# Order of the inner products, place of layer 2's constants, and an earlier branch flag in a four-layer fp32 kernel

## The chip, the cores and the metric

The kernel runs on one core of one Trainium2 chip. The metric is the time of one execution on the device in microseconds (us). A core has several engines, each with a queue that it works through in order: TensorE (PE in the profile) multiplies matrices, with its weight loads listed apart (PEld); VectorE (DVE), ScalarE (ACT) and GpSimd (POOL) work elementwise; SyncE (SP) here starts transfers. SBUF is the memory on the core that all of them read and write; PSUM holds what TensorE produces, in eight banks of 128 partitions x 512 fp32 words.

## What is computed

The input is a batch of 8 images with 512 channels of 32 x 32 positions, in fp32. Four layers follow each other:

```python
# layer 0: group norm, 8-head attention, three steps of an inner loop, projection
h = group_norm(x); q, k, v = split(qkv_w @ h + qkv_b)
hf = softmax(q.T k * 64 ** -0.5) @ v                  # per head, 64 channels
for _ in range(3):
    hf = hf + 0.1 * tanh(hf @ inl_w.T + inl_b)
x = x + proj_w @ hf + proj_b
# layer 1: one head, 64-wide q and k, 512-wide v
x = x + v1 @ softmax(q1.T k1).T
# layer 2: add bias, filter up by 2 (12 taps), leaky relu, filter down by 2 (12 taps)
x = down(leaky_relu(up(x + bias)) * sqrt(2))
# layer 3: 8 experts mixed per image, 1x1, 3x3 and 1x1 convolution with norms, relu, residual
x = relu(bn(conv1(relu(bn(conv3(relu(bn(conv1(x)))))))) + x)
```

## The kernel before

**Stages.** One program does everything. Layers 0 to 2 run image by image, with the result of layer 2 put aside in device memory; then layer 3 runs for all eight images. The Python code emits instructions in program order, and a scheduler then fixes the order in each engine's queue from that order of emission and from costs of its own. The kernel before and the changed one therefore differ in the queues by more than the lines edited. Whatever lies behind a waiting instruction in the queue of its engine waits with it.

**Products.** Each multiplication of a 512 x 512 weight with a 512 x 1024 activation (q, k, v, three inner steps `inl_0` to `inl_2`, proj in layer 0; v1 in layer 1: eight an image) is done in `product` (L382) in Strassen and Winograd's form: seven products of half the size, called P1, C11, U2, U3, C22, C21 and C12, instead of eight. The sums of activation quarters that it needs (tiles `T_...`) come from DVE in `quarter_sums` (L363), the sums of weight quarters from GpSimd in `weight_sums` for image 0, which also stores them for later images. Each of the seven is made in two halves, u = 0 and 1, of one PSUM bank each. P1 and C11 go into the pair of banks A (two tiles of one bank), the others into X (U2, U3, C21) and Y (C22, C12), each of which is one tile of two banks with the tag "scores". TensorE's matmuls for all of this are at L414. After both halves, `made` is called for each; it emits what takes the result out of PSUM:

- `channels` for q and k (ACT and DVE), `positions` for v and v1 (L478 to L495, with the adds of U2 and U3 to P1 at L488),
- `inner_step` for the inner loop: P1 is copied by ACT (L514), U2 and U3 are added to P1 by DVE (L519), C22, C21 and C12 are added to these (L523), ACT takes tanh (L508), and DVE adds a tenth of it to `hf` (L505),
- `residual` for proj, which adds into `x`.

`product` is a generator that yields after each of the seven; a caller can put other work between them.

**Attention in layer 0.** For each group of two heads and half of the positions, TensorE makes scores (L264: two matmuls of 64 rows each, r = 0 and 1, on the two halves of the array's rows), ACT the exponentials `e` (L613), DVE their running sum `acc` (L619), TensorE the weighted sum `av` (L628) and the column totals `total` (L638); DVE takes the reciprocal (L642) and multiplies it into `hf` (L643). GpSimd adds `acc` and `inv` into a tile `seen` (L645). The last of eight groups ends just before the first inner product, which needs its `hf`.

**Layer 1.** The first two parts of v1's product go out first, then the score matmuls (L264) two tiles at a time, with one more part of v1 after each:

```python
for steps in ((0,), (1, 2), (3, 4), (5, 6), (7,)):
    for t in steps:
        scores(t)
    next(values)
```

The exponentials are at L717; the weighted sum is a product of the same kind (L853, evacuated at L827), whose code the change does not touch.

**Layer 2's constants.** The filters are matmuls (L919 up, L940 down) with constant operators `up_op`, `up_left_op`, `dn_op`, `up63_op` and `dn63_op`. `layer2_constants()` (L132) makes them on the core out of the 12 taps, in some 370 small DVE instructions on tiles of 1 to 128 columns (L154 to L190), all in one scratch tile `setup`. It is called once, in layer 1 of image 0.

**The pools.** PSUM's eight banks are three pools: `ps_sc` (two tiles of two banks, the tag "scores"), `ps_tp` and `ps_mm` (two banks each). In SBUF the tag "tmp" has four buffers that the raw weight blocks of `weight` (`raw_kv`, `raw_inl`, `raw_proj`, ...), the exponentials and the tiles that hold P1, U2 and U3 share.

**The flag.** The softmax is computed without subtracting a maximum. At the end of the program `seen` is compared with a bound (L1167 to L1175), the count of values within it gives the flag `redo`, and the engines load it and branch: if it is set, the whole sequence runs again with shifts. In these runs it is not set.

Of the kernel before, what the change touches and what calls it, by code (L numbers as in the profile page):

```python
# [9 lines left out]
F32 = mybir.dt.float32  # L10
# [43 lines left out]
def tile_sequence(ctx: ExitStack, tc: tile.TileContext, a: dict, out: bass.AP, shifted: bool):  # L54
# [77 lines left out]
    def layer2_constants():  # L132

        setup = big_tile("setup", [P, CC * S])
        used = [0]

        def scratch(name, n):
            used[0] += n
            return setup[:, used[0] - n : used[0]]

        def iota(name, pattern, base, per_partition=0):
            t = scratch(name, pattern[0][1])
            nc.gpsimd.iota(
                t, pattern, base=base, channel_multiplier=per_partition,
                allow_small_or_imprecise_dtypes=True,
            )
            return t

        def placed(name, idx, taps):
            n = idx.shape[1]  # L150
            t, one = scratch(f"placed_{name}", n), scratch(f"one_{name}", n)
            for k in range(NTAP):
                dst = t if k == 0 else one
                nc.vector.tensor_scalar(  # L154
                    dst, idx, float(k), taps[:, k : k + 1], ALU.is_equal, ALU.mult
                )
                if k:
                    nc.vector.tensor_add(t, t, one)
            return t

        taps_up = scratch("taps_up", NTAP)
        nc.gpsimd.dma_start(taps_up, a["up_filter"].partition_broadcast(P))
        nc.vector.tensor_scalar_mul(taps_up, taps_up, 2.0)
        taps_dn = scratch("taps_dn", NTAP)
        nc.gpsimd.dma_start(taps_dn, a["down_filter"].partition_broadcast(P))

        part = iota("part", [[1, 1]], 0, 1)

        def rows_of(name, width):

            row, step = scratch(f"row_{name}", 1), scratch(f"step_{name}", 1)
            nc.vector.memset(row, 0.0)
            for k in range(width, P, width):
                nc.vector.tensor_scalar(step, part, float(k), None, ALU.is_ge)
                nc.vector.tensor_add(row, row, step)
            col = scratch(f"col_{name}", 1)
            nc.vector.scalar_tensor_tensor(col, row, float(-width), part, ALU.mult, ALU.add)
            return row, col

        def tap_index(name, n, step, base, mul, by):  # L180

            t = iota(f"ix_{name}", [[step, n]], base)
            add = scratch(f"add_{name}", 1)
            nc.vector.tensor_scalar_mul(add, by, float(mul))
            nc.vector.tensor_scalar_add(t, t, add)
            return t

        def outer(op, rows, cols):
            nr, ncol = rows.shape[1], cols.shape[1]
            nc.vector.tensor_tensor(  # L190
                op.rearrange("p (r c) -> p r c", c=ncol),
                rows.unsqueeze(2).to_broadcast([P, nr, ncol]),
                cols.unsqueeze(1).to_broadcast([P, nr, ncol]),
                ALU.mult,
            )

        in_c, in_r = rows_of("in", IR)
        ur = placed("ur", tap_index("ur", UR, -1, 17, -2, in_r), taps_up)
        outer(up_op, ur, placed("uc", tap_index("uc", UC, 1, 11, -2, in_c), taps_up))
        outer(
            up_left_op, ur, placed("ucl", tap_index("ucl", UC, 1, 11 - 2 * EDGE, -2, in_c), taps_up)
        )
        up_rr, up_cc = rows_of("up", UC)  # L210
        outer(
            dn_op,
            placed("dr", tap_index("dr", OR, 2, -6, 1, up_rr), taps_dn),
            placed("dc", tap_index("dc", OC, 2, 0, -1, up_cc), taps_dn),
        )
        in_c, in_r = rows_of("in63", 3)
        outer(
            up63_op,
            placed("ur63", tap_index("ur63", 1, 0, 10, -2, in_r), taps_up),
            placed("uc63", tap_index("uc63", 2 * W, 1, 5, -2, in_c), taps_up),  # L220
        )
        outer(
            dn63_op,
            placed("dr63", iota("dr63", [[2, 3]], 1), taps_dn),
            placed("dc63", tap_index("dc63", W, 2, 6, -1, part), taps_dn),
        )

        rim0 = tmp("rim0")
        nc.vector.memset(rim0, 0.0)
        for t in ypad:  # L230
            nc.gpsimd.dma_start(t[0 : 3 * W], rim0[0 : 3 * W])
            nc.gpsimd.dma_start(t[(H + 3) * W :], rim0[0 : 2 * W])
# [146 lines left out]
            nc.vector.tensor_sub(t[3][cc], t[1][cc], b21)  # L379
        return t  # L380

    def product(name, wt, src, sums_of, made, rows=False):  # L382

        banks = {
            "A": [bank(name=f"{name}_A{u}") for u in range(2)],
        }
        for key in "XY":
            two = ps_sc.tile([P, S], F32, tag="scores", name=f"{name}_{key}")  # L390
            banks[key] = [two[:, ts(u, HALF)] for u in range(2)]
# [6 lines left out]
        for what, key, part, data in order:  # L398
            part = wt[:, PARTS.index(part)]
            if isinstance(data, int):  # L400
                data = sums_of[data]
            else:
                data = [data[:, cc] for cc in range(2)]
            opens = what in ("P1", "U2", "C22")
            for u in range(2):
                ps = banks[key][u]
                for s in range(2 if rows else 1):
                    for cc in range(2):
                        if rows:
                            at = (2 * u + s) * P  # L410
                            dst, lhs, rhs = ps[:, ts(s, QR)], data[cc][:, at : at + P], part[:, cc]
                        else:
                            dst, lhs, rhs = ps, part[:, cc, ts(u, P)], data[cc]
                        nc.tensor.matmul(  # L414
                            dst, lhs, rhs, start=(opens and s == 0 and cc == 0),
                            stop=(cc == 1 and s == rows), skip_group_check=True,
                        )
            for u in range(2):
                made(what, u, banks[key][u])
            yield  # L420

    def all_of(gen):
        for _ in gen:
            pass
# [141 lines left out]
    def layer0(b, x, norm, w):  # L566
        h = group_norm(b, x, *norm)
        t = quarter_sums(f"h_{b}", h)
        if b == 0:
            for key in "kv":  # L570
                w[key] = weight_sums(key, *held[key], t[3][1][:, 0:1])
        q = big_tile(f"q_{b}", [P, CC, S])
        k = big_tile(f"k_{b}", [P, CC, S])
        v = big_tile(f"v_{b}", [P, SC, C])
# [73 lines left out]
        for t in range(0, n + 4, 2):  # L648
            for u in (t, t + 1):
                if u < n:  # L650
                    scores(u)
            for u in (t - 2, t - 1):
                if 0 <= u < n:
                    weighted(u)
            if t >= SC + 2 and (t - 2) % SC == 0:
                normalised((t - 2) // SC - 1)

        for it in range(3):
            t = quarter_sums(f"hf_{b}_{it}", hf, None if it else v)
            name = f"inl_{b}_{it}"  # L660
            all_of(product(name, w["inl"], hf, t, inner_step(name, hf)))
        if b + 1 < B:
            w["q"] = weight("q", b + 1)
        t = quarter_sums(f"hf_{b}_3", hf)
# [4 lines left out]
    def layer1(b, x, w, midway):  # L669
# [29 lines left out]
            )  # L699
        v = big_tile(f"v1_{b}", [P, SC, C])  # L700
        eT = [big_tile(f"eT_{b}_{sh}", [P, SC, HALF]) for sh in range(2)]
        if b == 0:
            layer2_constants()
        inv = small.tile([P, SC], F32, tag="inv1", bufs=2, name=f"inv1_{b}")
        accs = {}

# [31 lines left out]
            nc.gpsimd.tensor_add(seen[:, 0:4], seen[:, 0:4], inv[:, at])  # L738

        values = product(f"v1_{b}", w["v1"], x, t_x, positions(f"v1_{b}", v), rows=True)  # L740
        for _ in range(2):
            next(values)
        for steps in ((0,), (1, 2), (3, 4), (5, 6), (7,)):
            for t in steps:
                scores(t)
            next(values)
            if 4 in steps:
                totals(0)
        all_of(values)
# [336 lines left out]
    def mixed(b):  # L1086
# [10 lines left out]
                )  # L1097
        return wt

    z3 = {}  # L1100

    def freed(t):
# [8 lines left out]

    z_last = layer2(B - 1, halo, freed)
    z_next = z3[0]
    wt_next = mixed(0)
    route(B - 1, B)
    for b in range(B):
# [28 lines left out]
        for oc in range(CC):  # L1145
# [8 lines left out]
            for part in range(S // n):  # L1154
# [2 lines left out]
                    dst, ps[:, ts(part, n)], bn[2][0][:, oc : oc + 1], dst, ALU.mult, ALU.add  # L1157
                )
                nc.scalar.activation(dst, dst, AF.Relu, bias=bn[2][1][:, oc : oc + 1])
            nc.sync.dma_start(out[b, ts(oc, P), :], z[:, oc, :])  # L1160

    if shifted:
        return None

    within = tmp("within")  # L1167
    nc.vector.tensor_scalar(within, seen, BOUND, None, ALU.is_le)
    count = small.tile([P, 1], F32, tag="count", name="count")
    nc.vector.tensor_reduce(count, within, AX.X, ALU.add)  # L1170
    ps = bank(name="within")
    nc.tensor.matmul(ps[0:1, 0:1], count, ones[:, 0:1], start=True, stop=True)
    redo = small.tile([P, 1], mybir.dt.int32, tag="redo", name="redo")
    nc.vector.tensor_scalar(redo[0:1, :], ps[0:1, 0:1], P * HALF - 0.5, None, ALU.is_lt)
    return nc.values_load(redo[0:1, 0:1], min_val=0, max_val=1)  # L1175


def _layout(inp):
# [64 lines left out]
```

## Time and profile before

| what | value |
|---|---|
| time, median of 3 runs | 3966.25 us (3964.2 to 3972.21) |
| span of the profiled run | 3956.6 us |
| TensorE busy | 3873.8 us, 98% |
| VectorE busy | 2592.0 us, 66% |
| ScalarE busy | 1104.7 us, 28% |
| GpSimd busy | 437.9 us, 11% |
| DVE on `setup` (L154, L158, L174, L175), first and last start | 330.8 to 397.2 us |
| GpSimd's weight sums for proj, first and last start | 67.57 to 72.74 us |
| k of image 0, image 1, image 2 begins at | 43.45, 522.30, 978.89 us |

A line of the list of waits reads: engine, operation and line that waited, what it waited for, then the total in us, how many times, and the longest. A line of the timeline reads: start in us, length in us, engine, line, operation, output and inputs, shape, number of instructions drawn together, and in brackets the idle time of the engine before it and what ended it. An fp32 matmul of the program appears as two records. A line of the view of one tile reads: count, then the shortest, median and longest duration in ns, then the first and the last start.

### The profile page before, as it was taken

To read this page: it belongs to the slowest core of one execution; us is meant where nothing else is said; L and a number is where in the kernel's file an instruction comes from. 1 tells how busy PE (TensorE), PEld (TensorE's weight loads), DVE (VectorE), ACT (ScalarE), POOL (GpSimd) and SP (SyncE) were. 2 spreads that over 40 slices of the span, in tenths; PEclk is the share of its full clock that TensorE was granted. 3 is DMA by queue.
4 is the path that set the end of the run, shared out by engine and by line. 5 is a ranking of instruction groups with operands and counts; after the bars stand their busy time and mean duration, and the time that the engine had idled before them with its cause. 6 is when DMAs were issued, how large, how long until landed. Compare 5 with 4: busy or idle time off the path is not lost.

```text
span 3956.6 us, 37918 instructions
## 1 busy us (share of the span) xinstructions
PE 3873.8 (98%) x14630; PEld 2036.0 (51%) x14630; DVE 2592.0 (66%) x3690; ACT 1104.7 (28%) x1507; POOL 437.9 (11%) x310
## 2 busy tenths in 40 slices
PE   8998999999999999999999999999999999999998
PEld 4335753476435763367434764357534764346543
DVE  4779548764676647765486646765477655766885
ACT  1421214212332114212241223322142123321332
POOL 5310003000120003100030002200030001201000
PEclk9999999999999999999999999999999999999999
DMA  5002310113101310023101220013200131003432
GB/s 189 19 7 78 105 71 1 40 62 114 38 1 59 117 59 19 0 83 114 56 1 58 75 85 36 0 69 107 78 1 24 61 115 54 1 0 115 159 140 95
DMA packets 85214, 247.85 MB, mean 63 GB/s; under 512 B 10416, under 2 KB 32960, under 8 KB 78240
## 3 DMA queue, kind: packets, MB, share of 16 engines
q1 hardware_dynamic: 69136, 220.23, 15.6%
q10 hardware_dynamic: 13824, 12.59, 0.9%
q0 software_dynamic: 2064, 12.51, 0.8%
q8 instruction: 117, 1.92, 0.2%
q14 instruction: 73, 0.60, 0.0%
HBM read 185.40 MB, written 59.90 MB: 62 GB/s over the span
## 4 chain that ended last, share of the span: by engine, by line
PE 91%; DVE 6%; ACT 1%; DMA 1%; issue 1%; POOL 0%; ACTq 0%; SPq 0%; DVEq 0%; POOLq 0%
PE scores L264 13%; PE av L628 11%; PE inl_X L414 6%; PE dn L940 6%; PE up L919 5%; PE v_X L414 4%; PE inl_Y L414 4%; PE av_X L853 4%; PE inl_A L414 3%; PE c L1135 3%; PE v_Y L414 3%; PE av_Y L853 3%; PE av_A L853 2%; PE proj_X L414 2%; PE q_X L414 2%; PE k_X L414 2%
## 5 line engine op out<-in xcount | busy, mean ns | idle before, releaser
L613 ACT ACTIVATE e<-scores 128x1024 f32<-128x1024 f32 x512 | 497.4, 1022 | 583.0 <-PE scores L264 580.3
L619 DVE TENSOR_TENSOR acc<-acc,e 128x1024 f32<-128x1024 f32 x384 | 494.0, 1287 | 123.5 <-ACT e L613 103.4
L264 PE MATMUL scores<-q,k 64*128 64x512 f32 x2048 | 511.1, 616 | 6.0 <-DVE v L495 3.3
L628 PE MATMUL av<-e,v 128*64 128x512 f32 x2048 | 494.2, 605 | 0.0
L645 POOL TENSOR_TENSOR seen<-seen,acc 128x512 f32<-128x512 f32 x128 | 213.6, 1669 | 1565.0 <-DVE acc L619 1560.0
L264 PEld LDWEIGHTS scores<-q,k 64*128 64x128 f32 x2048 | 176.0, 186 | 333.1 <-ACT e L613 162.1
L628 PEld LDWEIGHTS av<-e,v 128*64 128x64 f32 x2048 | 124.9, 136 | 338.7 <-issue 336.4
L903 DVE SCALAR_TENSOR_TENSOR up<-up,leak 128x512 f32<-128x512 f32 (+1 forms) x264 | 174.5, 686 | 141.8 <-ACT leak L902 136.5
L940 PEld LDWEIGHTS dn<-dn_op,up 128*128 128x128 f32 (+1 forms) x2048 | 240.2, 192 | 44.0 <-issue 24.2
L940 PE MATMUL dn<-dn_op,up 128*128 128x126 f32 (+5 forms) x2048 | 244.7, 275 | 7.6 <-DVE up L903 6.8
L642 DVE RECIPROCAL inv<-total 128x512 f32<-128x512 f32 x64 | 214.7, 3355 | 0.0
L902 ACT ACTIVATE leak<-up 128x512 f32<-128x512 f32 (+1 forms) x264 | 150.1, 595 | 208.2 <-DVE up L903 131.0
L414 PE MATMUL inl_A<-hf,w_inl 128*128 128x512 f32 x384 | 178.0, 599 | 10.7 <-DVE hf L643 10.7
L919 PE MATMUL up<-halo,up_op 126*128 126x512 f32 (+1 forms) x384 | 182.6, 604 | 0.9 <-DVE up L903 0.8
L414 PE MATMUL inl_X<-T_hf,w_inl 128*128 128x512 f32 x384 | 175.2, 592 | 0.0
L645 POOL TENSOR_TENSOR seen<-seen,inv 128x512 f32<-128x512 f32 x64 | 125.2, 1956 | 416.9 <-DVE inv L642 416.9
L617 DVE TENSOR_TENSOR acc<-e,e 128x1024 f32<-128x1024 f32 x64 | 83.0, 1297 | 102.5 <-ACT e L613 102.5
L508 ACT ACTIVATE inl_U<-inl_U,inl_b 128x512 f32<-128x512 f32 x96 | 66.7, 718 | 287.4 <-DVE inl_U L523 287.4
L519 DVE TENSOR_TENSOR inl_U<-inl_X,inl_P 128x512 f32<-128x512 f32 x96 | 61.8, 685 | 111.4 <-PE inl_X L414 111.4
L737 POOL TENSOR_TENSOR seen<-seen,acc 128x512 f32<-128x512 f32 x16 | 23.4, 1461 | 987.7 <-DVE acc L729 921.5
L414 PEld LDWEIGHTS inl_A<-hf,w_inl 128*128 128x128 f32 x384 | 70.4, 190 | 110.2 <-issue 95.3
L1135 PE MATMUL c<-rim,mixed 128*128 128x512 f32 x288 | 124.9, 592 | 0.0
(302 smaller groups left out, 5779.0 us busy)
## 6 DMA issues: line engine op xcount, KB each, us to landing
halo<-ypad_u SPq DMA_DIRECT2D x128, 252.0 KB
halo<-ypad_u SPq DMA_DIRECT2D x128, 198.0 KB
w_v<-stored_u_v SPq DMA_DIRECT2D x14, 1792.0 KB
x<-in_x_dram SPq DMA_DIRECT2D x32, 512.0 KB
out_dram<-z SPq DMA_DIRECT2D x32, 512.0 KB
spill_u<-z SPq DMA_DIRECT2D x28, 512.0 KB
z<-spill_u SPq DMA_DIRECT2D x28, 512.0 KB
w_q<-stored_u_q SPq DMA_DIRECT2D x7, 1792.0 KB
```

The costliest lines, as they stand in the source:

```text
L264: nc.tensor.matmul(ps[r], k[r], q[r], start=True, stop=(shift is None))
L414: nc.tensor.matmul(dst, lhs, rhs, start=(opens and s == 0 and cc == 0), stop=(cc == 1 and s == rows), skip_group_check=True,)
L613: nc.scalar.activation(e, ps, AF.Exp, scale=HD ** -0.5)
L619: nc.vector.tensor_add(accs[g], accs[g], e)
L628: nc.tensor.matmul(avs[g][rows[r]], v[:, jc, ts(2 * oc + r, HD)], e[:, ts(r, HALF)], start=(jc == 0), stop=(jc == SC - 1),)
L642: nc.vector.reciprocal(inv, ps)
L645: nc.gpsimd.tensor_add(seen, seen, part)
L853: nc.tensor.matmul(ps[:, ts(s, QR)], left[:, j, at : at + P], right[:, j, :], start=(what in ("P1", "U2", "W") and s == 0 and j == 0), sto ...
L903: nc.vector.scalar_tensor_tensor(dst, ps, SQRT2, t, ALU.mult, ALU.max)
L919: nc.tensor.matmul(ps[i], op[0 : IR * n, :], halo.tile(t)[0 : IR * n, c + i, :], start=True, stop=True,)
L940: nc.tensor.matmul(rows[:, r0 - first : r1 + 1 - first, c0 : c1 + 1], up[t][0:k, c, ts(cc, P)], op[:, r0 - 4 * t + 3 : r1 + 4 - 4 * t, c0 ...
L1135: nc.tensor.matmul(banks[g].rearrange("p (h w) -> p h w", w=W), wt[:, at : at + P], h1[:, ky + 16 * g : ky + 16 * g + 16, kx : kx + W], st ...
```

## The change

There are four parts.

1. The first inner product of an image gets its pair of banks A from `ps_mm` and `ps_tp`, and its first half is emitted ahead of the totals of the last attention group (`normalised`), so that TensorE has work while the last sum and reciprocal are made.
2. In `product`, `made` is called after each half, and the generator yields after each half; only C12 still takes both of its halves at its end. Layer 1's loop takes twice as many steps of the generator, so that as many parts lie between its scores as before.
3. `layer2_constants()` works on GpSimd instead of DVE and is called in layer 0 of image 0, right after the sums of the weights of k and v, so that DVE is free in layer 1.
4. The flag `redo` is computed and loaded before layer 3 instead of after it; the stores of the output go out for each part as it is ready (halves for the last image, whole rows of 1024 for the others, as before).

```diff
@@ layer2_constants: all of its small operations @@
-                nc.vector.tensor_scalar(
+                nc.gpsimd.tensor_scalar(
                     dst, idx, float(k), taps[:, k : k + 1], ALU.is_equal, ALU.mult
                 )
                 if k:
-                    nc.vector.tensor_add(t, t, one)
+                    nc.gpsimd.tensor_add(t, t, one)
...
             for k in range(width, P, width):
-                nc.vector.tensor_scalar(step, part, float(k), None, ALU.is_ge)
-                nc.vector.tensor_add(row, row, step)
+                nc.gpsimd.tensor_scalar(step, part, float(k), None, ALU.is_ge)
+                nc.gpsimd.tensor_add(row, row, step)
...
-            nc.vector.scalar_tensor_tensor(col, row, float(-width), part, ALU.mult, ALU.add)
+            nc.gpsimd.tensor_scalar_mul(col, row, float(-width))
+            nc.gpsimd.tensor_add(col, col, part)
...
@@ product @@
-        banks = {
-            "A": [bank(name=f"{name}_A{u}") for u in range(2)],
-        }
+        banks = {"A": first_banks or [bank(name=f"{name}_A{u}") for u in range(2)]}
...
-            for u in range(2):
-                made(what, u, banks[key][u])
-            yield
+
+                for v in {"C12": ((), (0, 1))[u]}.get(what, (u,)):
+                    made(what, v, banks[key][v])
+                yield
@@ layer0 @@
                 w[key] = weight_sums(key, *held[key], t[3][1][:, 0:1])
+            layer2_constants()
...
-            if t >= SC + 2 and (t - 2) % SC == 0:
+            if t >= SC + 2 and (t - 2) % SC == 0 and t < n + 2:
                 normalised((t - 2) // SC - 1)
...
-            t = quarter_sums(f"hf_{b}_{it}", hf, None if it else v)
-            name = f"inl_{b}_{it}"
-            all_of(product(name, w["inl"], hf, t, inner_step(name, hf)))
+            name, t = f"inl_{b}_{it}", []
+            banks = None if it else [bank(p, f"{name}_A{u}") for u, p in enumerate((ps_mm, ps_tp))]
+            step = product(name, w["inl"], hf, t, inner_step(name, hf), first_banks=banks)
+            if it == 0:
+                next(step)
+                normalised(len(groups) - 1)
+            t += quarter_sums(f"hf_{b}_{it}", hf, None if it else v)
+            all_of(step)
@@ layer1 @@
-        if b == 0:
-            layer2_constants()
...
-        for _ in range(2):
+        for _ in range(4):
             next(values)
...
-            next(values)
+            for _ in range(2):
+                next(values)
@@ layer 3 @@
     z_next = z3[0]
+    redo = None if shifted else out_of_bounds()
...
-            nc.sync.dma_start(out[b, ts(oc, P), :], z[:, oc, :])
+                nc.sync.dma_start(out[b, ts(oc, P), ts(part, n)], dst)
```

`out_of_bounds` holds the comparison, the count and the load of the flag that stood at the end; its matmul writes to a bank of `ps_tp`.

More of the change, by code (lines that the diff above doesn't have):

```diff
@@ L162, in layer2_constants @@
         nc.gpsimd.dma_start(taps_up, a["up_filter"].partition_broadcast(P))
-        nc.vector.tensor_scalar_mul(taps_up, taps_up, 2.0)
+        nc.gpsimd.tensor_scalar_mul(taps_up, taps_up, 2.0)
         taps_dn = scratch("taps_dn", NTAP)
@@ L171, in rows_of @@
             row, step = scratch(f"row_{name}", 1), scratch(f"step_{name}", 1)
-            nc.vector.memset(row, 0.0)
+            nc.gpsimd.memset(row, 0.0)
             for k in range(width, P, width):
-                nc.vector.tensor_scalar(step, part, float(k), None, ALU.is_ge)
-                nc.vector.tensor_add(row, row, step)
+                nc.gpsimd.tensor_scalar(step, part, float(k), None, ALU.is_ge)
+                nc.gpsimd.tensor_add(row, row, step)
             col = scratch(f"col_{name}", 1)
-            nc.vector.scalar_tensor_tensor(col, row, float(-width), part, ALU.mult, ALU.add)
+            nc.gpsimd.tensor_scalar_mul(col, row, float(-width))
+            nc.gpsimd.tensor_add(col, col, part)
             return row, col
@@ L183, in tap_index @@
             add = scratch(f"add_{name}", 1)
-            nc.vector.tensor_scalar_mul(add, by, float(mul))
-            nc.vector.tensor_scalar_add(t, t, add)
+            nc.gpsimd.tensor_scalar_mul(add, by, float(mul))
+            nc.gpsimd.tensor_scalar_add(t, t, add)
             return t
@@ L189, in outer @@
             nr, ncol = rows.shape[1], cols.shape[1]
-            nc.vector.tensor_tensor(
+            nc.gpsimd.tensor_tensor(
                 op.rearrange("p (r c) -> p r c", c=ncol),
@@ L228, in layer2_constants @@
         rim0 = tmp("rim0")
-        nc.vector.memset(rim0, 0.0)
+        nc.gpsimd.memset(rim0, 0.0)
         for t in ypad:
@@ L380, in quarter_sums, with product @@
         return t
-    def product(name, wt, src, sums_of, made, rows=False):
-        banks = {
-            "A": [bank(name=f"{name}_A{u}") for u in range(2)],
-        }
+    def product(name, wt, src, sums_of, made, rows=False, first_banks=None):
+        banks = {"A": first_banks or [bank(name=f"{name}_A{u}") for u in range(2)]}
         for key in "XY":
@@ L1098, in mixed, with out_of_bounds @@
         return wt
+    def out_of_bounds():
+        within = tmp("within")
+        nc.vector.tensor_scalar(within, seen, BOUND, None, ALU.is_le)
+        count = small.tile([P, 1], F32, tag="count", name="count")
+        nc.vector.tensor_reduce(count, within, AX.X, ALU.add)
+        ps = bank(ps_tp, "within")
+        nc.tensor.matmul(ps[0:1, 0:1], count, ones[:, 0:1], start=True, stop=True)
+        redo = small.tile([P, 1], mybir.dt.int32, tag="redo", name="redo")
+        nc.vector.tensor_scalar(redo[0:1, :], ps[0:1, 0:1], P * HALF - 0.5, None, ALU.is_lt)
+        return nc.values_load(redo[0:1, 0:1], min_val=0, max_val=1)
     z3 = {}
@@ L1159, in tile_sequence @@
                 nc.scalar.activation(dst, dst, AF.Relu, bias=bn[2][1][:, oc : oc + 1])
-            nc.sync.dma_start(out[b, ts(oc, P), :], z[:, oc, :])
[L1162 to L1175, printed above, removed]
+                nc.sync.dma_start(out[b, ts(oc, P), ts(part, n)], dst)
+    return redo
 def _layout(inp):
```

## The prediction

> **What bounds the kernel now.** I read the busy shares first, then the chain that ended last, then the waits of TensorE, and last the timeline around each place that the change touches.
>
> ```profile
> PE 3873.8 (98%) x14630; PEld 2036.0 (51%) x14630; DVE 2592.0 (66%) x3690; ACT 1104.7 (28%) x1507; POOL 437.9 (11%) x310
> PE 91%; DVE 6%; ACT 1%; DMA 1%; issue 1%; POOL 0%; ACTq 0%; SPq 0%; DVEq 0%; POOLq 0%
> PE gn_mean L286 <- DVE mv L280: 10.9, 1, 10.9
> PE inl_A L414 <- DVE hf L643: 10.7, 7, 1.5
> PE v_X L414 <- DVE setup L174: 9.0, 1, 9.0
> PE total L638 <- DVE acc L619: 8.6, 8, 1.1
> ```
>
> TensorE is busy for 98% of the span: 3956.6 - 3873.8 = 82.8 us idle in all. Every other engine has room; GpSimd is idle for 89%. So a change gains only what it takes out of those 82.8 us, or out of matmul time, and loses whatever new gap it opens on TensorE. The three waits that the change aims at (10.7, 8.6, 9.0, each line: total, times, longest) can be seen in the list.
>
> How tight matmuls follow is needed below. These lines give start, length, engine, line and operation, and in brackets the idle time before:
>
> ```profile
> 727.50 6.17 PE L414 MATMUL inl_A<-hf,w_inl 128*128 128x512 f32 x14
> 727.70 1.29 DVE L523 TENSOR_TENSOR inl_U<-inl_Y,inl_U 128x512 f32<-128x512 f32 x2
> 732.09 0.68 DVE L377 TENSOR_TENSOR T_hf<-hf,T_hf 128x512 f32<-128x512 f32 x1
> 733.51 1.02 PE L414 MATMUL inl_X<-T_hf,w_inl 128*128 128x512 f32 x2
> ...
> 862.26 1.03 PE L853 MATMUL av_Y<-T,S 128*128 128x256 f32 x4
> 862.47 0.69 DVE L827 TENSOR_TENSOR av_U<-av_X,av_P 128x512 f32<-128x512 f32 x1
> 863.21 3.72 PE L853 MATMUL av_X<-T,S 128*128 128x256 f32 x16
> ...
> 813.24 1.13 PE L264 MATMUL scores<-qk 64*128 64x512 f32 x4
> 814.29 3.72 PE L414 MATMUL v_X<-w_v,T_x 128*128 128x256 f32 x16
> 817.95 1.99 PE L264 MATMUL scores<-qk 64*128 64x512 f32 x8
> 819.86 3.72 PE L414 MATMUL v_X<-w_v,T_x 128*128 128x256 f32 x16
> ```
>
> A written 128x512 matmul is two records of 0.43 us (14 records from 727.50 to 733.51), so 0.86 us; a 128x256 one is 0.43. A half of a product (one u) is 1.72 us.
>
> **The Trainium skill.** "Perfetto Trace Analysis", section "Tensor Engine Instruction", says that the matmul's end in a profile is a model, and that GpSimd, DVE and ACT are strictly first in, first out. The trace agrees on the first: four records from 862.26 issue until 862.26 + 4 x 0.215 = 863.12 but are drawn to 863.29, beyond the next one's start, so short stalls don't show as waits. "GPSIMD Engine Reference", section 3.1, puts two software dispatch steps into each GpSimd instruction and a tensor_tensor at 1.96 times DVE's time; here a 128x512 add takes 1.26 us there against 0.69 on DVE, 1.8 times. Its section 1 has GpSimd's way into SBUF shared with DVE; here the 128x4 add (L738) takes 0.20 to 1.17 us. "TensorE: Matmul & The Clock Gate", section "The mechanism", lets matmuls in different row groups run at once; here a pair of 64-row score matmuls takes 1.05 us (813.24 to 814.29) and two pairs 1.91 us, where four written 128x512 matmuls in turn would take 3.44.
>
> **Part 1, inner loop first.** In the order of the changed kernel P1's first half stands between the last av and total_7, and its second half behind it, in banks of two other pools. The wait of total on acc (8.6 us for all images) and of inl_A on hf (10.7) have one and two halves of work in front of them, 1.72 us each, against waits of 1.1 and 1.5. I count both as gone: **-19.3 us**.
>
> **Part 2, reads after each half.** `made` now runs after each u, and the generator yields there. X and Y are one tile of two banks each, and in the changed order every second half written to X or Y carries a wait on DVE's read of the first half, where before both halves were written and then read.
> - Short waits. With one other matmul in between, this wait exists already in the weighted sum of layer 1: av_X at 863.21 against 863.12, 0.09 us. I count 21 of these an image (three each in q, k, v, three inner products, v1): 1.9 us. v's second U3 half has nothing in front of it and waits for matmul drain, add and back: 0.16 + 0.05 + 0.69 + 0.05 = 0.95. Together 2.85 us an image, **+22.8**.
> - The filler is used up. What the order puts into those gaps is the next product's P1 (four written matmuls, 3.44 us). Before, P1 and C11 (14 records left after C12, 6.0 us) covered the chain from C12's end through the U adds, tanh, steps and T_hf: 727.66 to 732.77, 5.1 us. Now that chain is about 5.3 us (C22's step stands ahead of the adds), and in front of the next U2 are six matmuls (5.16 us) in the second inner product, but only C11's four (3.44 us) in the third and in proj: about 0.3 + 2.0 + 2.0 us. P1, moved forward, also waits about 0.25 us for the step of hf (or the residual of x) in three places. 5.05 us an image, **+40.4**.
> - Split score pairs. In layer 1, score pairs 1, 3, 5 and 7 now have half a v1 product between their two matmuls and lose their overlap. Before: 1.05 + 3 x 1.91 + 1.07 = 7.85 us. After: one pair (1.05), five lone ones (about 0.88, a written matmul) and three groups of three (two row slots, 1.85): 11.0. **+25.2** for 8 images.
>
> **Part 3, constants on GpSimd.** About 373 small instructions (87 + 77 on one column, the rest on 8 to 128) leave DVE. What they cost now is read from the periods of two like images, from k_0's start to k_1's (43.45 to 522.30, 478.85 us) and on to k_2's (522.30 to 978.89, 456.59): 22.3 us, of which the 9.0 above is one piece. **-22**.
>
> But `layer2_constants()` now stands behind the weight sums of k and v, and in the changed order of GpSimd all 373 lie ahead of w_proj's sums, whose raw block fills one of four buffers of the tag "tmp". v_0's U3 add on DVE waits for the last read of it (L358), as do the second U3 matmuls and the first exponentials. Before, that was never late:
>
> ```profile
> 28.09 0.18 POOL L354 COPY w_k<-T_h 128x1 f32<-128x1 f32 x1 [2.46 <-DVE T_h L379]
> 28.24 1.48 POOL L359 TENSOR_SCALAR w_k<-raw_kv 128x512 f32<-128x512 f32 x1
> 72.74 1.25 POOL L358 TENSOR_TENSOR w_proj<-w_proj 128x512 f32<-128x512 f32 x1
> 83.11 1.29 DVE L488 TENSOR_TENSOR v_U<-v_X,v_P_hi 128x512 f32<-128x512 f32 x2 [3.95 <-issue]
> ```
>
> The sum was read at 74.0 and the buffer wanted at 83. A small GpSimd instruction follows the last in 0.15 us at best (28.09 to 28.24); the 128x4 add has a minimum of 0.20 and a median of 0.48 beside a busy DVE. I take 0.2, 373 x 0.2 = 75, plus 6 for those that share SBUF with a working DVE. They start near 44 (k's and v's sums end at 40.5, the taps land 2.8 after issue): 44 + 81 + 6.5 (w_inl's five sums, in between) + 1.2 (two DMA issues) + 5.3 (w_proj's sums to L358) = 138. TensorE wants the buffer at about 81.5: **+56**. Bounds: 0.15 each gives 113, +31; 0.3 each gives 175, +93. Behind the waiting add, DVE's queue holds all of v_0, and TensorE all of attention, so nothing fills the hole.
>
> **Part 4, branch flag and out by halves.** Some 1.2 us of DVE work move to the start of layer 3, where DVE has room; the register load no longer follows the last store, and the last image's store goes in halves. The tail after the last matmul is some 10 us (3946.3 to 3956.6), most of it evacuation and landing, which stay: **-1**.
>
> Sum: -19.3 + 22.8 + 40.4 + 25.2 - 22 + 56 - 1 = +102; 3966 + 102 = **4068 us**.
>
> **Rivals.**
> - GpSimd's small instructions cost 0.27 to 0.3 us (for: the 0.48 median; against: once TensorE stands, DVE idles and shares nothing). Stall 82 to 93: about 4100.
> - The constants are hidden after all, by cheaper instructions or a buffer wanted later: 4068 - 56 = 4012. For: GpSimd is idle for 89%; against: even at 0.15 the queue is 31 us late.
> - The half waits cost next to nothing, since the scheduler did fill in. Only the GpSimd hole is left: 3966 - 19 - 22 - 1 + 56 = 3980. Against: the filler was already in use as cover.
> - Faster: neither hole nor half waits, 3966 - 19 - 22 - 1 = 3924. For: TensorE's listed waits do shrink; against: needs both arguments above to fail.
>
> **Chances.** The forecast 0.60, slow GpSimd 0.14, hidden constants 0.10, cheap halves 0.08, faster 0.08. The range 4000 to 4125 takes in the first three (0.84), and the bounds of the stall, 4068 - 25 and 4068 + 37. Faster by over 0.2% 0.09 (the last case and a little of the fourth), the same 0.02, slower 0.89.
>
> **What would show it.** Right: a wait of PE v_X on DVE v_U of some 56 us near 80 to 138; no wait of total on acc or inl_A on hf; waits of inl_X and proj_X on T_hf of about 2 us, sixteen times; score matmuls of layer 1 at 0.88 us alone; image 1's period about 456.6 + 11 - 2.4 = 465 us. Wrong: GpSimd's last constant before 70 us, or a period of image 1 at or below 456.6.

## The result, and the profile after

The changed kernel takes 4142.88 us (median of 6 runs, 4138.27 to 4146.98) against 3965.38 us of the kernel before: ratio 1.0444, 95% interval 1.043 to 1.0457. It is 177 us slower; the forecast was 102 slower, with 4125 as the upper end.

The engines' busy time and the chain that ended last, of the changed kernel:

```profile
PE 3963.0 (96%) x14630; PEld 2032.1 (49%) x14630; DVE 2582.1 (62%) x3328; ACT 1115.2 (27%) x1507; POOL 525.8 (13%) x675
PE 87%; DVE 7%; POOL 3%; ACT 1%; issue 1%; DMA 1%; SPq 0%; DVEq 0%; ACTq 0%; POOLq 0%
```

GpSimd is on the chain now, with 3%. The span grew by 188.6 us (3956.6 to 4145.2), but TensorE's listed idle time only by 99 (82.8 to 182.2): with the same 14630 records its busy time grew by 89. A matmul's drawn length can reach past the next one's start (863.29 against 863.21 in the forecast's lines), so short gaps are covered, and matmuls that no longer overlap are counted one after the other. Lost time has to be sought in start times as well as in waits.

TensorE's waits in the changed kernel (total, times, longest):

```profile
PE v_X L414 <- DVE v_U L489: 90.3, 8, 84.8
PE inl_X L414 <- DVE v L378: 14.2, 8, 2.1
PE proj_X L414 <- DVE T_hf L378: 13.4, 8, 1.8
PE inl_X L414 <- DVE T_hf L378: 13.3, 8, 1.7
```

The waits of `total` on `acc` and of `inl_A` on `hf` are gone (8.6 and 10.7 before), and so is v_X on `setup` (9.0). Four others stand in their place or have grown. The first is nearly all one hole of 84.8 us in image 0. The timeline there (start, length, engine, line, and in brackets the idle time before and its cause):

```profile
163.16 0.29 POOL L191 TENSOR_TENSOR up_op<-setup 128x64 f32<-128x64 f32 x1
163.42 1.26 POOL L356 TENSOR_TENSOR w_proj<-raw_proj 128x512 f32<-128x512 f32 x1
167.34 1.26 POOL L358 TENSOR_TENSOR w_proj<-w_proj,raw_proj 128x512 f32<-128x512 f32 x1
168.63 0.69 DVE L489 TENSOR_TENSOR v_U<-v_X,v_P_hi 128x512 f32<-128x512 f32 x1 [86.07 <-POOL w_proj L358]
169.38 3.58 PE L414 MATMUL v_X<-w_v,T_h 128*128 128x256 f32 x8 [84.77 <-DVE v_U L489]
```

Read upward it is the predicted chain: TensorE waits for DVE's read of v_X, DVE for the buffer of `raw_proj`, whose last reader is GpSimd's L358, and that stands behind the last constant.

Where the 188.6 us of the two profiled spans lie is told by equal points in both timelines, the start of the last layer 2 matmul of an image and the first convolution matmul of layer 3:

| stretch | before | after | difference | forecast |
|---|---|---|---|---|
| start to image 0's last layer 2 matmul | 498.65 | 578.74 | +80.1 | +43 |
| images 1 to 7, to layer 3's first matmul | 3208.47 | 3319.10 | +110.6 | +60 |
| layer 3 to the end | 249.48 | 247.36 | -2.1 | -1 |

Image 2, which holds no large single wait in either kernel, splits the second row by stage:

| stretch of image 2 | before | after | difference | forecast |
|---|---|---|---|---|
| last layer 2 matmul of image 1 to first scores (q, k, v) | 71.79 | 74.81 | +3.0 | +1.8 |
| to layer 1's first scores (attention, inner loop, proj) | 242.79 | 247.78 | +5.0 | +3.4 |
| to layer 2's first matmul (layer 1) | 73.91 | 79.97 | +6.1 | +3.4 |
| layer 2 | 67.78 | 67.80 | 0.0 | 0 |

Each of the three losses lies where it was forecast, and each is larger. Seven times the 14.1 us of image 2 are 99 of the 110.6. The rest lies in images 1, 4 and 5, which lost 3.3, 4.9 and 3.8 us more than image 2. Each of them has a stretch in which the granted TensorE clock was about half: 0.50 from 794 to 797 us, 0.51 from 2418.5 to 2425.5, 0.53 from 2896.4 to 2900. Other kernels' traces have such stretches in other places (the last version below has 0.54 from 2711.5 to 2715.2), and no run shows what sets them off, so they are not counted as the change's. The two profiled spans differ by 11 us more than the medians do.

### The profile page after: what moved, and what is told of

Its sections match the earlier page's. It is cut to its first block, busy times and chain, and to the rows that moved or that the text cites. A ratio compares the mean times of both kernels' runs of the same rounds, so it can differ in the third digit from the quotient of the medians.

```text
span 4145.2 us, 37873 instructions
## 1 busy us (share of the span) xinstructions
PE 3963.0 (96%) x14630; PEld 2032.1 (49%) x14630; DVE 2582.1 (62%) x3328; ACT 1115.2 (27%) x1507; POOL 525.8 (13%) x675
## 4 chain that ended last, share of the span: by engine, by line
PE 87%; DVE 7%; POOL 3%; ACT 1%; issue 1%; DMA 1%; SPq 0%; DVEq 0%; ACTq 0%; POOLq 0%
PE scores L265 13%; PE av L630 11%; PE inl_X L414 6%; PE dn L948 5%; PE up L927 4%; PE av_X L861 4%; PE v_X L414 4%; PE inl_Y L414 3%; PE c L1157 3%; PE v_Y L414 3%; PE av_A L861 3%; PE inl_A L414 3%; PE av_Y L861 3%; PE v_A L414 2%; PE proj_X L414 2%; PE q_X L414 2%
## 5 line engine op out<-in xcount | busy, mean ns | idle before, releaser
L948 PE MATMUL dn<-dn_op,up 128*128 128x126 f32 (+5 forms) x2048 | 249.6, 278 | 12.6 <-DVE up L911 11.9
L414 PE MATMUL inl_X<-T_hf,w_inl 128*128 128x512 f32 x384 | 189.7, 610 | 13.3 <-DVE T_hf L378 13.3
L414 PE MATMUL v_X<-w_v,T_h 128*128 128x256 f32 x384 | 96.9, 393 | 90.3 <-DVE v_U L489 90.3
L414 PEld LDWEIGHTS inl_X<-T_hf,w_inl 128*128 128x128 f32 x384 | 67.7, 189 | 123.5 <-issue 57.4
L414 PEld LDWEIGHTS v_X<-w_v,T_h 128*128 128x128 f32 x384 | 71.4, 193 | 109.8 <-DVE v_U L489 98.6
```

What stands on the lines that cost most here:

```text
L414: nc.tensor.matmul(dst, lhs, rhs, start=(opens and s == 0 and cc == 0), stop=(cc == 1 and s == rows), skip_group_check=True,)
L948: nc.tensor.matmul(rows[:, r0 - first : r1 + 1 - first, c0 : c1 + 1], up[t][0:k, c, ts(cc, P)], op[:, r0 - 4 * t + 3 : r1 + 4 - 4 * t, c0 ...
```

## The experiments

The profiled lines of the changed kernel and of the experiments have slightly different line numbers; the tiles' names are the same.

**The constants back on DVE.** The changed kernel, with layer 2's constants as they were:

```diff
-            layer2_constants()          # layer 0, all on nc.gpsimd
...
+        if b == 0:
+            layer2_constants()          # layer 1, all on nc.vector
```

> The changed kernel with layer 2's constants made by DVE again, at their old place in layer 1; all else as changed. Theory 1 (the 84.8 us hole in image 0 is GpSimd's queue of constants ahead of the weight sums for proj, and TensorE restarts after it at half its clock): the hole and the slow restart go, about 4 us of it, and the 22 us on DVE in layer 1 come back: 4143 - 85 - 4 + 22 = about 4076. Rival (the hole comes from the new order of v's halves, and GpSimd only happens to end then): the hole stays and 22 us are added, about 4165.

Measured: 4073.61 us, 69 less than the changed kernel. The hole is gone; in its windows from 84 to 169 and from 169 to 174 us TensorE was busy for 83.7 and 5.0 us. Compare the same windows of the changed kernel (columns: window, its length, busy time of PE, PEld, DVE, ACT and POOL with counts, granted TensorE clock, DMA share, GB/s):

```profile
84.00:169.00 85.00, 0.61 (x3) 0.19 (x1) 0.37 (x1) 0.00 (x0) 72.52 (x261) 0.52 0.10 38
169.00:174.00 5.00, 4.62 (x14) 3.84 (x15) 1.71 (x3) 0.00 (x0) 1.48 (x2) 0.64 0.54 228
167.00:172.00 5.00, 2.62 (x6) 2.17 (x7) 1.38 (x2) 0.00 (x0) 3.48 (x4) 0.50 0.20 85
172.00:180.00 8.00, 8.00 (x36) 6.70 (x36) 2.77 (x4) 0.00 (x0) 0.00 (x0) 0.96 0.43 179
```

While GpSimd works, the other engines all but stand. Afterwards the granted clock is 0.50 up to 172 us and 0.96 from there to 180; the 0.64 is a mean over both. The first eight records of v_X take 3.41 us (169.38 to 172.79), where eight took 1.83 in image 2 (1111.28 to 1113.11, shown further down). That slow restart costs 1.6 us: from the resumed U3 half to the first scores are 12.33 us in image 0 (169.38 to 181.71) and 10.74 in image 2 (1116.84 to 1127.58). The expectation had 4 for it.

Theory 1 holds: 84.8 us of hole and 1.6 of restart go, and 17 to 18 come back on DVE (by the timeline 14.6 in layer 1 and 3.7 in layer 2 of image 0), where 22 were expected. In this kernel the constants meet the half-wise reads in layer 1 of image 0: there v_X waits 13.7 us for a v_U that stands behind `setup` in DVE's queue.

**Reads after both halves.** One line of the changed kernel:

```diff
-                for v in {"C12": ((), (0, 1))[u]}.get(what, (u,)):
+                for v in ((), (0, 1))[u] if key in "XY" else (u,):
```

> The changed kernel, but results of the two-bank tiles X and Y are read after both halves are written, as before; P1 and C11 are still read half by half. Theory 2 (the loss of about 14 us in every image comes from the halves waiting for reads within one two-bank tile, and from what the scheduler moves into those gaps): the period of images 1 to 6 goes back from 470 to about 456 us, and the time to about 4143 - 8 x 14 = 4030, nearly all above the kernel before being the hole in image 0. Rival (the period grew from the first inner product's new place or from the order of layer 1's loop, which stay here): about 4140.

Measured: 4019.21 us, 124 less than the changed kernel, and 1.0136 (1.0119 to 1.0153) of the kernel before. All three per-image losses go: in image 2 the stretches are 71.8, 241.5 and 73.9 us. The half-wise reads of the two-bank tiles are thus the cause of the three losses in images 1 to 7, since the new order of the first inner product and of layer 1's loop is still there. What remains above the kernel before is the hole, 83.5 us here and 1.6 for the restart, less the gains of the other parts.

**The same in v1 alone, and in the inner loop and proj alone.**

```diff
+                for v in ((), (0, 1))[u] if key in "XY" and name.startswith("v1") else {"C12": ((), (0, 1))[u]}.get(what, (u,)):
```

> The changed kernel with X and Y read after both halves in v1 alone, which puts layer 1's score pairs together again. Theory 2a (lone score matmuls cost 1.05 us, as much as a pair, since each also pays about 0.2 us for starting after a matmul of another row count): the stretch from layer 1's first scores to the first up goes from 80.0 to about 74 us, and the time to 4143 - 8 x 6 = about 4095. Rival, the size in the forecast (3.15 us an image): 4118.

Measured: 4100.83 us, 42 less than the changed kernel; image 2's layer 1 takes 74.8 instead of 80.0 us. That fits theory 2a and not the forecast's size. The cause can be read from TensorE's timeline, first of the kernel before, image 2:

```profile
1269.82 1.13 PE L264 MATMUL scores<-qk 64*128 64x512 f32 x4
1270.88 3.72 PE L414 MATMUL v_X<-w_v,T_x 128*128 128x256 f32 x16
1274.53 1.99 PE L264 MATMUL scores<-qk 64*128 64x512 f32 x8
```

and then of the changed kernel:

```profile
1375.36 2.06 PE L265 MATMUL scores<-qk 64*128 64x512 f32 x4
1377.35 1.99 PE L414 MATMUL v_X<-w_v,T_x 128*128 128x256 f32 x8
1379.28 1.12 PE L265 MATMUL scores<-qk 64*128 64x512 f32 x2
1380.33 1.99 PE L414 MATMUL v_X<-w_v,T_x 128*128 128x256 f32 x8
1382.25 1.98 PE L265 MATMUL scores<-qk 64*128 64x512 f32 x6
```

A lone score matmul (1379.28, two records) takes 1.05 us to the next start, as long as a whole pair did (1269.82 to 1270.88). Each change between scores and v_X costs as well: 8 records of v_X take 1.93 us (1377.35 to 1379.28) where 8 x 0.215 = 1.72. The first pair no longer overlaps either (1375.36 to 1377.35, 1.99 us): its second matmul needs keys that ACT writes until 1376.25. That loss of 0.9 us is not v1's. In this experiment the first pair still lies apart (1.98 us), which is why 74.8 and not 73.9 is reached; in the next one it is together again (1.06 us).

The next experiment changes the same line, with `name[:3] in ("inl", "pro")` in place of the test for `v1`:

> The changed kernel with X and Y read after both halves in the three inner products and proj alone. Theory 2b (the next product's P1, moved into the gaps, is missing as cover for T_hf's chain, and each short wait costs 0.19 us, twice what was forecast): the waits of inl_X and proj_X on T_hf, 26.7 us in all, go, and the time goes to 4143 - 8 x 6 = about 4095. Rival (the chain itself is longer, with DVE's adds in another order): the waits stay, 4130 or more.

Measured: 4080.45 us, 62 less than the changed kernel. The waits of inl_X and proj_X on T_hf (26.7 us) are gone, and the stretch to layer 1's first scores is 241.5 us. That fits theory 2b: the chain was not longer, its cover had been used up. In the changed kernel the cover can be seen to end:

```profile
1311.92 3.60 PE L414 MATMUL inl_A<-hf,w_inl 128*128 128x512 f32 x8
1312.24 1.28 DVE L524 TENSOR_TENSOR inl_U<-inl_Y,inl_U 128x512 f32<-128x512 f32 x2
1316.44 0.68 DVE L378 TENSOR_TENSOR T_hf<-hf,T_hf 128x512 f32<-128x512 f32 x1
1317.18 1.12 PE L414 MATMUL inl_X<-T_hf,w_inl 128*128 128x512 f32 x2 [1.67 <-DVE T_hf L378]
```

Eight records of C11 (3.44 us) lie over a chain of 4.9 us, 1312.24 to 1317.12; before, it was 5.1 (727.66 to 732.77 in the forecast's lines). With 42 from v1 and 62 from the inner loop and proj, some 20 of the 124 are left for q, k and v. The table has 8 x 3.0 = 24, and the single runs spread by more than that difference (up to 14 us).

**The first inner product's place alone.** The kernel before with part 1 (half of P1, then `normalised`, then the rest). P1 and C11 are also read half by half here in every product; X and Y are read as before:

```diff
+            if it == 0:
+                next(step)
+                normalised(len(groups) - 1)
```

> The kernel before with part 1 alone: the first inner product's first half ahead of the last totals, in banks of two other pools. Theory 3 (the wait is handed on: the chain from the last sum of exponentials through total, reciprocal and hf to the T sums is as long as before, so that what total and inl_A no longer wait for, inl_X waits for): total and inl_A wait for nothing, inl_X about 1.5 to 2 us an image, and the time is 3965 - 5 = about 3960. Rival, the step of the forecast (both waits gone for nothing): 3946.

Measured: 3951.61 us, ratio 0.9965 (0.9953 to 0.9976): 9 to 19 us faster, between the two theories' numbers. The wait is handed on, but not whole. The timeline of this experiment, image 2:

```profile
1162.85 0.69 DVE L649 TENSOR_TENSOR hf<-av,inv 128x512 f32<-128x512 f32 x1
1163.46 1.32 DVE L511 SCALAR_TENSOR_TENSOR hf<-inl_C,hf 128x512 f32<-128x512 f32 x1
1164.70 0.68 DVE L377 TENSOR_TENSOR v<-hf,v 128x512 f32<-128x512 f32 x1
1165.43 1.98 PE L414 MATMUL inl_X<-v,w_inl 128*128 128x512 f32 x4 [1.73 <-DVE v L377]
```

`total` and `inl_A` wait for nothing; `inl_X` waits 1.73 us for the T sums, which lie in `v`'s tile. That is 13.8 us in all against 19.3 for the two waits removed. DVE does a step of C11 (1163.46, 1.32 us) ahead of the sum that TensorE needs. By the timeline the gain is 1.3 us an image (242.79 to 241.5), 10 in all. Not all of it is the new place: in the kernel before, C11 of v1 in image 2 waits for ACT's copy of P1 and its first two starts come 0.51 us late (1267.27 to 1268.22); read half by half, 0.07 are left. So some 0.4 of the 1.3 us, 3.5 in all, go with the earlier reading of P1, and some 7 with the new place.

**The flag alone.** The kernel before with part 4.

> The kernel before with part 4 alone: the flag computed and loaded ahead of layer 3, the last image stored in halves. Forecast: the stretch from the last TensorE work to the end gets about 1 to 2 us shorter, 3963 to 3964. Rival (the load of the flag holds a queue that layer 3 needs): 3967 or more.

Measured: 3964.79 us, ratio 0.9997 (0.9988 to 1.0005): nothing that can be told from no change. The profiled stretch from layer 3's first matmul to the end went from 249.5 to 246.8 us, much as in the changed kernel (247.4), but a gain of that size doesn't show in the times.

**The constants on GpSimd, at a time when nothing needs it.** The kernel before with part 3, but held back until image 0's attention is over. Only a true dependency keeps them there, since the order is the scheduler's, and so their scratch tile first takes a copy of the last `hf`:

```diff
-        setup = big_tile("setup", [P, CC * S])
+        setup = const.tile([P, 640], F32, name="setup")
+        nc.gpsimd.tensor_copy(setup[:, 0:512], held)        # held = the last hf
+        nc.gpsimd.tensor_copy(setup[:, 512:640], held[:, 0:128])
```

> The kernel before with part 3 alone, but GpSimd's constants held back (by a copy from the last hf into their scratch tile, now a tile of its own) until attention of image 0 is over, where GpSimd has some 130 us before its next sums. Theory 1b (moving the constants is worth DVE's 22 us, if they stand behind every weight sum): no hole in image 0, 3966 - 22 = 3944. Rival (373 small GpSimd instructions slow DVE by their use of SBUF, or hold layer 1's buffers): 3955 or more.

Measured: 3956.29 us, ratio 0.9979 (0.9971 to 0.9986): about 9 us faster, which is the rival's number. Image 0's hole in v is gone, and layer 1 no longer waits for `setup`. But GpSimd needs until 370.3 us, some 12.5 us too long:

```profile
370.05 0.29 POOL L193 TENSOR_TENSOR up_op<-setup 128x64 f32<-128x64 f32 x1
370.30 1.26 POOL L740 TENSOR_TENSOR seen<-seen,acc 128x512 f32<-128x512 f32 x1
371.60 1.29 DVE L807 TENSOR_TENSOR T<-v 128x512 f32<-128x512 f32 x2 [12.49 <-POOL seen L740]
377.68 1.97 PE L761 MATMUL xT<-ident,x 128*128 128x128 f32 x8 [12.59 <-DVE y L762]
```

The same thing again with other names: a sum into `seen` stands behind the constants, holds the buffer of `acc`, DVE's next tile needs that buffer, and TensorE waits 12.6 us.

GpSimd is also slower here than in the changed kernel. Its small instructions have nearly the same shortest and median time, but a longest one of 1.4 us against 0.54 (from the view of the tile `setup`, which is shown for the changed kernel below):

```profile
L156 POOL TENSOR_SCALAR setup<-setup x108: 287/361/1402, 250.2 to 369.1; 128x16 f32<-128x16 f32 x24, 128x9 f32<-128x9 f32 x12, 128x3 f32<-128x3 f32 x12, 128x32 f32<-128x32 f32 x12
```

All 35 that took over 0.6 us overlap a DVE instruction with two inputs in SBUF, such as `T_hf<-hf` or `acc<-acc,eT`. The 62 with such an overlap take 0.76 us in the mean, the other 311 take 0.26, beside a working DVE or not. By that count the overlap added some 31 us, more than the 12.5 that were missing. In the changed kernel no small instruction overlaps a DVE instruction of this kind. The overlap is read from the trace; no run takes it away alone.

**What was left standing, together.** Part 1, both halves before a read, the flag early, the constants held back:

> What the runs left standing, put together: the first inner product's half ahead of the last totals, X and Y read after both halves as before, the constants on GpSimd held back until attention of image 0 is over, the flag before layer 3. From the single parts: 3966 - 15 (part 1 alone) - 22 - 1 = about 3928. Rival (part 1 and the constants compete for GpSimd or for the same DVE time): 3940 or more.

Measured: 3945.42 us, ratio 0.9952 (0.9935 to 0.9968). That is 17 us more than expected and in the rival's range; the wait is still there and is most of it (13.7 us).

**Fewer GpSimd instructions.**

```diff
...
-            for k in range(width, P, width):
-                nc.gpsimd.tensor_scalar(step, part, float(k), None, ALU.is_ge)
-                nc.gpsimd.tensor_add(row, row, step)
+            ge = iota(f"ge_{name}", [[-width, len(range(width, P, width))]], -width, 1)
+            nc.gpsimd.tensor_scalar(ge, ge, 0.0, None, ALU.is_ge)
+            nc.vector.tensor_reduce(row, ge, AX.X, ALU.add)
```

> The version of the run before, with 126 of the 373 GpSimd instructions (the sums over is_ge, one column each) replaced by three rows of iota, one is_ge and one DVE sum each, which give the same numbers. There a wait of 13.7 us of TensorE was left in layer 1 of image 0, since a DVE subtraction needs a buffer that GpSimd's sum into seen reads, and that sum stood behind the constants. If GpSimd's time for the queue is the cause, 126 x about 0.26 = 33 us fewer end the queue ahead of that sum: the wait goes and the time is 3945 - 13 = about 3932. Rival (the subtraction waits for something else): the wait stays, 3945.

Measured: 3933.67 us (3931.35 to 3934.41), ratio 0.9909 (0.9892 to 0.9925). TensorE's waits in this version:

```profile
PE inl_X L416 <- DVE v L379: 14.2, 8, 2.1
PE gn_mean L288 <- DVE mv L282: 11.0, 1, 11.0
PE dn L955 <- DVE up L918: 10.6, 9, 5.6
PE scores L266 <- DVE v L503: 3.3, 8, 0.4
```

The wait in layer 1 is gone, and GpSimd's last constant starts at 335.3 instead of 370.1 us, so the length of GpSimd's queue was its cause. This version beats both kernels, by 35 us and by 209 us.

## Why the prediction was wrong in size

**Right: the direction and both main mechanisms.** The chain through `tmp`, L358 and v's U3 add, the half-wise waits in X and Y, the used-up cover of P1, the split score pairs: each is in the trace where it was forecast, and each goes when its part is undone.

Put together, the measured terms make up the change: 84.8 + 1.6 us for the hole, 8 x 14.1 in the images, less 22 on DVE, come to 177. What failed is the size of three terms: the hole was forecast 29 us too short, the halves' losses some 35 too small (88 against 8 x 15.4, which is 14.1 and the 1.3 that part 1 gains), and part 1's gain 9 too large. The 1.6 of the restart was not forecast.

**The step that failed first: "I take 0.2" us for a small GpSimd instruction.** The view of the tile `setup` in the changed kernel (duration in ns: shortest, median, longest; then first and last start):

```profile
L154 POOL TENSOR_SCALAR setup<-setup x108: 290/358/544, 52.1 to 162.2; 128x16 f32<-128x16 f32 x24, 128x3 f32<-128x3 f32 x12, 128x32 f32<-128x32 f32 x12, 128x9 f32<-128x9 f32 x12
L158 POOL TENSOR_TENSOR setup<-setup x99: 183/214/322, 54.6 to 162.8; 128x16 f32<-128x16 f32 x22, 128x3 f32<-128x3 f32 x11, 128x32 f32<-128x32 f32 x11, 128x9 f32<-128x9 f32 x11
L174 POOL TENSOR_SCALAR setup<-setup x63: 208/217/231, 46.2 to 143.3; 128x1 f32<-128x1 f32 x63
L175 POOL TENSOR_TENSOR setup<-setup x63: 182/194/216, 47.8 to 143.6; 128x1 f32<-128x1 f32 x63
```

The four rows are 108 x 0.358 + 99 x 0.214 + 63 x 0.217 + 63 x 0.194 = 86 us of median duration for 333 instructions, 0.26 each, and a step adds the gap to the next: from one start to the next L154 and L175 have medians of about 0.44 and 0.18, and all constants together take 108 us by starts, 0.29 each, where the forecast had 81. The two-operation tensor_scalar with a scalar per partition, 108 of the 373, costs most, and the forecast had priced it from a one-column copy and a small add. From 46.2 to 163.4 are 117 us, with w_inl's sums, the rim's memset and its stores in between; the four stores of the rim, some 0.6 us each, were not counted at all. Together that makes 84.8 us of hole against 56. The rival "slow GpSimd" (0.27 to 0.3 us, hole of 82 to 93) described this part. Its reason, SBUF shared with a busy DVE, does not explain it in this kernel: most of these instructions ran while DVE stood, and the 51 that ran beside a DVE instruction took 0.25 us in the mean, the other 323 0.27. With the constants held back, beside DVE's SBUF sums, the reason does fit (35 instructions of over 0.6 us).

**The second: the short waits at 0.09 us and the lone score matmuls at 0.88.** Both were read from the first start alone. In the changed kernel's v of image 2:

```profile
1110.33 1.03 PE L414 MATMUL v_Y<-w_v,T_h 128*128 128x256 f32 x4
1110.53 0.69 DVE L489 TENSOR_TENSOR v_U<-v_X,v_P 128x512 f32<-128x512 f32 x1 [0.60 <-PE v_X L414]
1111.28 1.99 PE L414 MATMUL v_X<-w_v,T_h 128*128 128x256 f32 x8
1113.11 1.03 PE L414 MATMUL v_Y<-w_v,T_h 128*128 128x256 f32 x4
```

v_X starts 0.95 us after v_Y instead of 0.86 (0.09, as forecast), and then its eight records take 1.83 instead of 1.72 (1111.28 to 1113.11): another 0.1 between the first and the second record. Such a wait is 0.19 us. This was in the trace of before, just behind the lines that the forecast shows: from 863.21 the 16 records of av_X take 3.56 us to the next start at 866.77, where 16 x 0.215 = 3.44. With 0.1 more at nine waits, q, k and v come to 2.7 us an image instead of 1.8, of 3.0 measured; four of the nine, in q and k, were longer (0.25 to 0.26). In layer 1 the same price is paid at every change between scores and v1, of which there are more now, and a lone score matmul with one at each side takes 1.05 us instead of 0.88. The first pair's lost overlap, 0.9 us, was not in the forecast; it goes with the reads in the inner loop and proj. Together 6.1 instead of 3.4.

**The third: part 1 at -19.3.** It gave some 10 by the timeline, 9 to 19 by the times. The forecast checked that the matmuls put in front are long enough for each wait removed, but not when the T sums behind the same chain end. `inl_X` now ends that chain, with 14.2 us.

**Right in size:** the two T_hf waits (2.0 forecast, 1.7 in the list, 1.8 by starts), the 0.95 us of v's second U3 half (0.95 by starts), the tail (no measurable change). The constants' 22 us on DVE are real too, but were got only in the last version: from part 1 alone to it the ratio goes from 0.9965 to 0.9909, which is 22 us of 3966 (the two intervals leave some 8 us either way), and image 0 takes 20.9 us less in the profiled runs (499.31 to 478.44). Two small terms were too large: 0.3 us in the second inner product was 0.11, and 0.25 in three places for P1 was 0.18, 0.18 and 0.24. And two readings were off without consequence: the last reader of `raw_proj` in the kernel before is L357, which ended at 72.8, and not L358, which ended at 74.0; and some of the small tiles have 3 columns, not 8 and more.

## What to carry to other kernels

Idle time of an engine is not room for a job of its length: what counts is what stands behind the job in that engine's queue, and which buffers those instructions release. Here 117 us on an engine idle for 89% of the span held a 1.3 us sum, and with it everything. When work is cut into finer pieces inside one tracked tile, look for the false waits first, and then at what a scheduler moves into the gaps, since it may be the cover of a longer chain. And price a wait by the starts of the two or three instructions after it, not of the first alone.

## What the runs showed of the hardware

- A lone 64-row score matmul between 128-row ones takes 1.05 us to the next start (1379.28 to 1380.33 in the changed kernel), as long as two of them on different halves of the rows (1269.82 to 1270.88 before). 0.19 of it lies at the two changes of row count.
- A wait of TensorE that is met 0.09 us late costs 0.19 (1111.28 in the changed kernel): there is a second gap of 0.1 us after the first record that follows it.
- After 85 us without matmuls the granted clock was 0.50 for some 3 us more and 0.96 from 172 to 180 us, which cost 1.6 us.
- GpSimd's two-operation tensor_scalar with per-partition scalars took 0.30 us on one column and 0.53 on 64, tensor_tensor 0.19 and 0.32. One column costs more than half of what 64 do, so most of such an instruction's price does not come from its columns.
- Small GpSimd instructions took 0.26 us in the mean, and 0.76 (up to 1.40) where they overlapped a DVE instruction with two inputs in SBUF (constants held back, 62 of 373).
